# Sums' reciprocals and inverse norms of the attention layer: spread over channels by DMA from HBM instead of by matmuls

## The chip, the cores and the metric

The kernel runs on one core of one Trainium2 chip. A core has a tensor engine (PE in the profile, with its weight loads as PEld), a vector engine (DVE), a scalar engine (ACT), a general engine (POOL, GpSimd) and a queue processor that issues DMA transfers (SP). The metric is the device time of one execution in microseconds (us). All data is 32-bit floating point.

## The reference, cut to what matters

The network runs four layers over two images (batch 2) of 512 channels and 64 x 64 positions. Only the first layer is touched here. It is an attention with eight heads of 64 channels. Every position attends to its own 3 x 3 neighbourhood (nine "taps") and to 256 pooled tokens; queries and keys are scaled to unit length per head and position:

```python
q_norm = q / max(norm(q), 1e-12)                      # per head and position
q_scaled = (q_norm + query_embedding) * softplus(temperature)
k_l = k / max(norm(k), 1e-12)                         # per head and position
attn = softmax(concat([q_scaled . k_local (9 taps), q_scaled . k_pool (256 tokens)]))
a_local, a_pool = attn[..., :9], attn[..., 9:]
lt = q_norm @ learnable_tokens + learnable_bias + a_local
x_local = sum over taps of lt[tap] * v_local[tap]
x_pool = a_pool @ v_pool
out = (x_local + x_pool) @ W_proj + b_proj
```

Two kinds of numbers exist once per head and position and have to be multiplied onto all 64 channels of the head: the **inverse norms** of q and k, and the **reciprocal of the softmax's sum**, with which x_pool is scaled. Channels lie on the partitions (128 partitions are two heads), so each such number has to be brought from one row to 64 partitions. How that is done is what the change concerns.

## The kernel before

The first layer works on units: 128 channels (two heads) by 1024 positions, in two halves of 512 positions (TB). There are 4 x 4 = 16 units per image. A step `i` of the main loop works on several units in different stages at once. Each stage is a generator; `in_turn` runs every stage up to its next `yield`, in the order of the list, so a step is some ten "ticks" of interleaved work:

```python
for i in range(-4, units + 1):
    k, q, ahead, u, before = (unit(i + n) for n in (4, 3, 1, 0, -1))
    streams, ended = [], []
    stages = [self.norms(streams, ended)]
    if ahead is not None:
        stages.append(self.tap_products(ahead))     # DVE: q * shifted k, nine taps
    if u is not None:
        stages.append(self.attend(u))               # scores, exp, values, sums
    if before is not None:
        stages.append(self.weigh(before))           # nine taps of v, weighted
    if ahead is not None:
        stages.append(self.tap_sums(ahead))         # PE: sums over channels
    ...
    stages.append(self.projections(k, q, values, streams))   # ticks 6..9: k, k, q, q
    stages.append(self.normed(ended))               # inverse norms onto k and q
    ...
    in_turn(*stages)
```

`projections` writes the raw k or q (L2014) and its square (L2016) for four streams: k and q, two halves each. A step later `norms` sums the squares per head on PE, transposes them so that the positions lie on partitions, takes the inverse root on DVE in short instructions, and transposes back into `rows`, which holds the inverse norms of stream s in partitions 32 s and 32 s + 1:

```python
def norms(self, streams, ended):
    before, self.pending = self.pending, streams
    if not before:
        return
    yield
    ps = self.bank()
    for s in range(4):
        nc.tensor.matmul(ps[32 * s:32 * s + 32, :], self.cst[:, C_E32:C_E32 + 32],
                         before[s % len(before)][4], start=True, stop=True)       # L2048
    rows = wp.tile([P, TB], F32, name="n_rows")
    nc.scalar.copy(rows, ps)                                                      # L2051
    yield
    ...                            # L2055: transposes; L2062 to L2070: inverse root on DVE
    yield
    yield
    yield
    ps = self.bank()
    for t in range(NT):
        nc.tensor.transpose(ps[:, t * P:(t + 1) * P], self.wide[:, t, :], self.net.ident)  # L2076
    rows = wp.tile([P, TB], F32, name="n_rows")
    nc.scalar.copy(rows, ps)                                                      # L2078
    ended += [(s, rows[32 * s:32 * s + 2, :], *a) for s, a in enumerate(before)]
    yield
```

`normed` brings two rows onto 128 partitions with a matmul of contraction length 2 against a matrix of ones and zeros, and DVE multiplies k and q by the result in PSUM:

```python
def normed(self, ended):
    for _ in range(5):
        yield
    for which in "kq":
        mine = [(e, self.bank()) for e in ended if e[2] == which]
        for (s, rows, *_), ps in mine:
            nc.tensor.matmul(ps, self.cst[32 * s:32 * s + 2, C_ROW:C_ROW + P], rows,
                             start=True, stop=True)                               # L2090
        for (_, _, _, u, j, part, _), ps in mine:
            ...
            nc.vector.tensor_tensor(out, part, ps, ALU.mult)                      # L2098
        yield
    if mine:
        self.learned(mine[-1][0][3])     # L2111: PE on q, then ACT makes the scaled q
    yield
```

`attend` ends with the sums (L2205, L2209 on PE), their reciprocals (L2230), and the weights `el` of the taps, which go to HBM (`spread`, L2237) and come back one tap at a time, each row read onto 64 partitions (`fetch_tap`, L2247: two transfers of 256 KB per tap, into a ring of three `taps` buffers). `weigh` scales the pooled part by the reciprocals with the same kind of matmul, then works off nine taps:

```python
def weigh(self, u):
    out, R = self.out.pop(u), self.recip
    self.fetch_tap(2)
    yield
    banks = [self.bank() for _ in range(2)]
    for j, ps in enumerate(banks):
        q = slice(64 * j, 64 * j + 2)
        nc.tensor.matmul(ps, self.cst[q, C_ROW:C_ROW + P], R[q, :], start=True, stop=True)  # L2260
    for j, ps in enumerate(banks):
        o = out[:, j * TB:(j + 1) * TB]
        nc.vector.tensor_tensor(o, o, ps, ALU.mult)                               # L2263
    for k in range(9):
        ...
            nc.scalar.copy(ps, part)                                              # L2270
        ...
            nc.vector.tensor_tensor(part, vx (shifted), ps, ALU.mult)             # L2273
        nc.gpsimd.tensor_tensor(out, out, self.taps[k % 3], ALU.add)              # L2277
        if k + 3 < 9:
            self.fetch_tap(k + 3)
        if k < 8:
            yield
    nc.sync.dma_start(self.yd[:, cc, lo:lo + self.UT], out)                       # L2283
    yield
```

The PSUM tiles of all these parts come from one pool of five banks (`bank()`). All DMA of this layer is issued from one queue, in order, by SP.

Of the kernel before, what the change touches and what calls it, by code (L numbers as in the profile page):

```python
# [8 lines left out]
F32 = mybir.dt.float32  # L9
I32 = mybir.dt.int32  # L10
AF = mybir.ActivationFunctionType
ALU = mybir.AluOpType
# [3 lines left out]
P = 128  # L16
# [4 lines left out]
TB = 512  # L21
# [3 lines left out]
HD = 64  # L25
# [1674 lines left out]
class Local:  # L1700
# [9 lines left out]
    def __init__(self, net, X, Y, sp_scale, d, wp, yp, pp, ppt, pps):  # L1710
        self.net, self.nc, self.vec, self.cst = net, net.nc, net.vec, net.cst
        self.X, self.sp_scale, self.d = X, sp_scale, d
        self.wp, self.pp, self.ppt, self.pps = wp, pp, ppt, pps
        nc, new = self.nc, lambda shape, name: wp.tile(shape, F32, name=name)

        self.yd = yp.tile([P, KC, N], F32, name="yd")
        self.wd = yp.tile([3, P, KC, C], F32, name="wd")
        self.rows = cycle([yp.tile([P // 2, self.UT], F32, name=f"rows{i}") for i in range(2)]).__next__

        R = W + 2  # L1720
        self.kx_flat = flat = Y.rearrange("p k n -> p (k n)")
# [24 lines left out]
        self.w_sr = qs[:, :KC * C].rearrange("p (kc o) -> p kc o", kc=KC)  # L1746
        self.fold = flat[:, :6144].rearrange("p (i kc o) -> p i kc o", i=3, kc=KC)
        self.kp = new([P, KC, NK], "kp")
        self.vp = new([P, 2, C], "vp")
        self.qn = new([P, self.UT], "qn")  # L1750
        self.w3 = new([P, 3, KC, P], "w3")
        self.sq = [new([P, TB], f"sq{i}") for i in range(4)]
        self.half = new([P, 32], "mhalf32")
        self.wide = new([P, NT, P], "wide")
        self.qb = new([P, KC], "qe_scaled")
        self.bias = {i: new([P, KC], "b_" + i) for i in "qkv"}
        self.raw = {"k": self.kraw, "q": self.qn}
# [21 lines left out]
    def run(self):  # L1779
# [11 lines left out]
        for i in range(-4, units + 1):  # L1791
            k, q, ahead, u, before = (unit(i + n) for n in (4, 3, 1, 0, -1))
            streams, ended = [], []
            stages = [self.norms(streams, ended)]
            if ahead is not None:
                stages.append(self.tap_products(ahead))
            if u is not None:
                stages.append(self.attend(u))
            if before is not None:
                stages.append(self.weigh(before))  # L1800
            if ahead is not None:
                stages.append(self.tap_sums(ahead))

            values = ([ahead] if i >= self.UN - 1 and ahead is not None
                      else {-4: [0], -3: [1, 2], -2: [3]}.get(i, []))
            stages.append(self.projections(k, q, values, streams))
            stages.append(self.normed(ended))
            if i < -2:
                stages.append(islice(heads, 12 if i == -4 else None))
            if i == units - 3:  # L1810
                stages.append(self.fetch_output())
            if i > units - 3:
                stages.append(self.output(i - units + 2))
            in_turn(*stages)
# [223 lines left out]
    def norms(self, streams, ended):  # L2038


        nc, wp = self.nc, self.wp
        before, self.pending = self.pending, streams
        if not before:
            return
        yield
        ps = self.bank()
        for s in range(4):
            nc.tensor.matmul(ps[32 * s:32 * s + 32, :], self.cst[:, C_E32:C_E32 + 32],  # L2048
# [21 lines left out]
            nc.vector.scalar_tensor_tensor(dst, a, 1.5, y, ALU.add, ALU.mult)  # L2070
        yield
        yield
        yield
        ps = self.bank()
        for t in range(NT):
            nc.tensor.transpose(ps[:, t * P:(t + 1) * P], self.wide[:, t, :], self.net.ident)  # L2076
        rows = wp.tile([P, TB], F32, name="n_rows")
        nc.scalar.copy(rows, ps)  # L2078
        ended += [(s, rows[32 * s:32 * s + 2, :], *a) for s, a in enumerate(before)]
        yield  # L2080

    def normed(self, ended):

        nc = self.nc
        for _ in range(5):
            yield
        for which in "kq":
            mine = [(e, self.bank()) for e in ended if e[2] == which]
            for (s, rows, *_), ps in mine:
                nc.tensor.matmul(ps, self.cst[32 * s:32 * s + 2, C_ROW:C_ROW + P], rows, start=True,  # L2090
                                 stop=True)
            for (_, _, _, u, j, part, _), ps in mine:
# [5 lines left out]
                nc.vector.tensor_tensor(out, part, ps, ALU.mult)  # L2098
            yield
        if mine:  # L2100
            self.learned(mine[-1][0][3])
        yield

    def learned(self, u):
# [65 lines left out]
    def attend(self, u):  # L2170
# [64 lines left out]
        self.spread = self.rows()  # L2235
        for j in range(2):
            nc.sync.dma_start(self.spread[:, j * TB:(j + 1) * TB], el[j * HD:(j + 1) * HD, :])  # L2237
        self.fetch_tap(0)
        yield
        self.fetch_tap(1)  # L2240
        yield

    def fetch_tap(self, k):

        at = 32 * (k % 2) + 2 * k
        for h in range(2):
            self.nc.sync.dma_start(self.taps[k % 3][h * HD:(h + 1) * HD, :],  # L2247
                                   bcast(self.spread[at + h], 0, HD))

    def weigh(self, u):  # L2250

        nc = self.nc
        cc, y0 = u // self.UN, u % self.UN * self.UY
        out, R = self.out.pop(u), self.recip
        self.fetch_tap(2)
        yield
        banks = [self.bank() for _ in range(2)]
        for j, ps in enumerate(banks):
            q = slice(64 * j, 64 * j + 2)
            nc.tensor.matmul(ps, self.cst[q, C_ROW:C_ROW + P], R[q, :], start=True, stop=True)  # L2260
        for j, ps in enumerate(banks):
            o = out[:, j * TB:(j + 1) * TB]
            nc.vector.tensor_tensor(o, o, ps, ALU.mult)  # L2263
        for k in range(9):
            dy, dx = divmod(k, 3)
            parts = [self.taps[k % 3][:, j * TB:(j + 1) * TB] for j in range(2)]

            banks = [self.bank() for _ in range(2)]
            for ps, part in zip(banks, parts):
                nc.scalar.copy(ps, part)  # L2270
# [6 lines left out]
            nc.gpsimd.tensor_tensor(out, out, self.taps[k % 3], ALU.add)  # L2277
# [167 lines left out]
```

## Time and profile before

| | before |
|---|---|
| median of 3 runs | 5462.01 us (5449.31 to 5468.27) |
| span of the profiled execution | 5449.6 us |
| mean granted PE clock | 0.969 of full |
| one full step of the first layer (486.57 to 532.43, and the two after it) | 45.86 us each |
| first layer, first image | about 50 to 1100 us of the span |
| first layer, second image | about 2750 to 3800 us |

The page gives busy time per engine, the costliest groups of instructions by line, and the DMA queues. Below, the step of 45.86 us is read from the timeline: each row has its start, its length, the engine, the line of the kernel, the operation with output and input tiles, the count, and in brackets what the engine had been idle for. A 32-bit matmul of 512 columns leaves two matmul records, so a projection of four matmuls is a row of x8. Starts of successive rows on PE are the surer measure of what a row costs there, as the recorded ends are modelled.

### The profile page before, as it was taken

The page shows a single profiled execution, that of the slowest core. Times are in us where ns is not written, and L with a number is a line of the kernel's source. Part 1 is how long each engine was busy: PE and PEld are TensorE (multiplying, and loading weights), DVE is VectorE, ACT ScalarE, POOL GpSimd, SP SyncE. Part 2 cuts the span into 40 slices and gives each one's busy share as a digit, 9 for nine tenths or more (in the row PEclk, how much of TensorE's full clock was granted, in tenths as well). Part 3 has the DMA queues.
Part 4 walks back from the last instruction along what each step waited for, and adds up shares of the span by engine and source line. Part 5 has one row for each costly group of instructions (what it writes and reads, how often), then busy time and mean ns, then how long its engine had stood idle before and what let it go on. Part 6 is the DMA issues. An engine that isn't in the chain of part 4 may idle for free. (4 is left out here: it accounts for less than half of the span.)

```text
span 5449.6 us, 51666 instructions
## 1 busy us (share of the span) xinstructions
PE 5161.0 (95%) x18891; PEld 2254.2 (41%) x18891; DVE 3144.7 (58%) x3918; ACT 1793.0 (33%) x3409; POOL 1803.2 (33%) x1198
## 2 busy tenths in 40 slices
PE   7999999999988899999999999998999889999998
PEld 4423332554333344544444333335543334445443
DVE  3256667745679633565532566676456895334565
ACT  1245555233212233212212455542432131332221
POOL 0025556401310045444400355554012101554443
PEclk9999999999989999999989999999999899999999
DMA  3024445500000000211110344455000000000111
GB/s 141 2 62 122 128 126 154 153 18 24 1 1 0 1 1 1 82 35 57 51 55 2 81 126 125 124 154 154 1 24 0 1 0 1 1 8 20 38 36 42
DMA packets 113563, 293.27 MB, mean 54 GB/s; under 512 B 17234, under 2 KB 30034, under 8 KB 111252
## 3 DMA queue, kind: packets, MB, share of 16 engines
q1 hardware_dynamic: 113300, 289.88, 18.1%
q8 instruction: 151, 2.47, 0.2%
q14 instruction: 112, 0.92, 0.1%
HBM read 241.32 MB, written 48.50 MB: 53 GB/s over the span
## 5 line engine op out<-in xcount | busy, mean ns | idle before, releaser
L133 PE MATMUL mm<-big,w 128*128 128x512 f32 x2560 | 1188.4, 609 | 5.2 <-DVE late L2230 5.1
L133 PEld LDWEIGHTS mm<-big,w 128*128 128x128 f32 x2560 | 467.8, 191 | 687.4 <-issue 590.3
L2277 POOL TENSOR_TENSOR late<-late,big 128x1024 f32<-128x1024 f32 x192 | 454.7, 2368 | 298.6 <-DVE big L2273 285.3
L1265 POOL TENSOR_TENSOR total<-prob 128x512 f32<-128x512 f32 x128 | 159.6, 1269 | 759.3 <-ACT prob L1262 759.3
L1182 PE MATMUL acc<-big,dg 128*128 128x512 f32 x704 | 320.0, 613 | 59.0 <-DVE big L697 25.9
L1624 POOL TENSOR_SCALAR qf_sum<-qf,ksum_ratio 128x512 f32<-128x512 f32 x128 | 198.8, 1562 | 511.1 <-ACT qf L1674 353.8
L1437 POOL TENSOR_TENSOR big<-big 128x512 f32<-128x512 f32 x224 | 277.8, 1271 | 235.0 <-ACT big L1428 235.0
L2198 POOL TENSOR_TENSOR late<-late 128x512 f32<-128x512 f32 x128 | 160.6, 1276 | 487.1 <-ACT late L2187 448.2
L697 DVE TENSOR_TENSOR big<-big 128x3968 f32<-128x3968 f32 x72 | 308.8, 4289 | 6.9 <-ACT big L698 0.9
L2273 DVE TENSOR_TENSOR big<-big,mm 128x512 f32<-128x512 f32 x384 | 254.7, 679 | 85.1 <-ACT mm L2270 84.3
L1428 ACT ACTIVATE big<-mm,ed 128x256 f32<-128x256 f32 x512 | 193.7, 488 | 276.5 <-DVE top L1424 248.8
L2270 ACT COPY mm<-big 128x512 f32<-128x512 f32 x384 | 220.6, 594 | 161.4 <-DMA big<-rows 123.7
L1362 PE MATMUL mm<-proj,k 64*128 64x256 f32 x2048 | 268.9, 393 | 0.9 <-ACT k L1329 0.9
L1282 DVE RECIPROCAL recip<-psD 128x512 f32<-128x512 f32 x64 | 214.9, 3357 | 87.2 <-PE psD L1279 87.2
L1655 PE MATMUL mm<-k,w 128*128 128x512 f32 x512 | 242.0, 612 | 14.1 <-DVE k L1648 14.1
L1583 DVE TENSOR_REDUCE tops<-mm 128x2 f32<-128x512 f32 x256 | 161.5, 684 | 160.2 <-PE mm L1362 159.9
L1262 ACT ACTIVATE prob<-mm 128x512 f32<-128x512 f32 x256 | 132.0, 605 | 364.4 <-PE mm L1259 359.2
L1362 PEld LDWEIGHTS mm<-proj,k 64*128 64x128 f32 x2048 | 206.5, 188 | 105.7 <-issue 90.1
L2138 DVE TENSOR_TENSOR prod<-qs,big 128x1024 f32<-128x1024 f32 x192 | 230.5, 1215 | 30.7 <-PE tap L2151 29.1
L2277 POOL TENSOR_TENSOR late<-late,tap 128x1024 f32<-128x1024 f32 x96 | 226.5, 2360 | 64.4 <-DVE tap L2273 45.7
L133 PE MATMUL mm<-big,big 128*128 128x512 f32 x512 | 238.9, 629 | 0.0
L2151 PE MATMUL tap<-prod,cst 128*32 128x512 f32 x768 | 226.7, 612 | 9.9 <-DVE prod L2138 9.8
(364 smaller groups left out, 8300.2 us busy)
## 6 DMA issues: line engine op xcount, KB each, us to landing
big<-rows SPq DMA_DIRECT2D x384, 256.0 KB
tap<-rows SPq DMA_DIRECT2D x192, 256.0 KB
yd<-late SPq DMA_DIRECT2D x32, 512.0 KB
lost_all<-lost SPq DMA_DIRECT2D x128, 128.0 KB
out<-big SPq DMA_DIRECT2D x64, 256.0 KB
big<-in_W_kv SPq DMA_DIRECT2D x8, 1024.0 KB
rows<-late SPq DMA_DIRECT2D x64, 128.0 KB
big<-yd SPq DMA_DIRECT2D x16, 512.0 KB
```

Of the source, the lines that this page charges most:

```text
L133: self.nc.tensor.matmul(ps, w[:, kc, :], X[:, kc, blk * TB:(blk + 1) * TB], start=(kc == 0), stop=(kc == KC - 1))
L697: nc.vector.tensor_tensor(o, a, b, ALU.max)
L1182: nc.tensor.matmul(accs[b], dg, src[:, b * TB:(b + 1) * TB], start=(j == 0), stop=(j == 6))
L1282: nc.vector.reciprocal(r, psD)
L1362: nc.tensor.matmul(pS[h][i][:, t, :], k[lo:lo + HD, tok:tok + P], proj[lo:lo + HD, :], start=True, stop=True)
L1437: nc.gpsimd.tensor_tensor(a, a, part, ALU.add)
L1655: nc.tensor.matmul(ps, self.wo[:, kc, oc * P:(oc + 1) * P], qs[:, kc, :], start=(kc == 0), stop=(kc == KC - 1))
L2138: self.nc.vector.tensor_tensor(self.prods[k % 3].rearrange("p (y x) -> p y x", x=W), qs, self.kx[:, y + dy:y + dy + self.UY, dx:dx + W], A ...
L2151: nc.tensor.matmul(ps[32 * q:32 * q + 32, :], self.cst[:, C_TAPW + 16 - 2 * k:C_TAPW + 48 - 2 * k], self.prods[k % 3][:, j * TB:(j + 1) * ...
L2270: nc.scalar.copy(ps, part)
L2273: nc.vector.tensor_tensor(part.rearrange("p (y x) -> p y x", x=W), self.vx[:, y:y + self.UY // 2, dx:dx + W], ps.rearrange("p (y x) -> p y ...
L2277: nc.gpsimd.tensor_tensor(out, out, self.taps[k % 3], ALU.add)
```

## The change

The row-to-64-partitions matmuls are replaced by the way that the tap weights already take: out to HBM, and back with each row read onto 64 partitions, then an ACT copy into the same PSUM bank from which DVE multiplies.

For the reciprocals no write is added. Row 20 + h of what is already written to `spread` holds exp(0) times the reciprocal plus zero, which is the reciprocal of head h. So the reciprocals become a tenth "tap", numbered 0, and the nine taps become 1 to 9. For the norms there is a new HBM buffer `roots` of 2 x 4 x 512 numbers (two of them in turn); the read-back lands in the `sq` buffers, whose squares have been used by then. The norms' stage starts without its first `yield` and has one `yield` less before the second transposes, and it now stands after the projections in a tick instead of at the front. The load of the last weights into `sq` is moved to a later tick, as `sq` is in use for longer. It is meant to take work off PE.

```diff
+        self.roots = cycle([yp.tile([2, 4, TB], F32, name=f"roots{i}") for i in range(2)]).__next__
-        self.sq = [new([P, TB], f"sq{i}") for i in range(4)]
+        self.squares = new([P, 4, TB], "sq")
+        self.sq = [self.squares[:, i, :] for i in range(4)]
 ... run
-            stages = [self.norms(streams, ended)]
+            stages = []
 ...
-            stages.append(self.normed(ended))
+            stages += [self.norms(streams, ended), self.normed(ended)]
 ... fetch_output
-        for _ in range(3):
+        for _ in range(7):
             yield
 ... norms
-        yield
         ps = self.bank()
         for s in range(4):
 ...
         yield
         yield
-        yield
         ps = self.bank()
         for t in range(NT):
 ...
-        ended += [(s, rows[32 * s:32 * s + 2, :], *a) for s, a in enumerate(before)]
+        roots = self.roots()
+        for h in range(2):
+            nc.sync.dma_start(roots[h], rows[h:P:32, :])
+        for s in range(0, len(before), 2):
+            for h in range(2):
+                nc.sync.dma_start(self.squares[h * HD:(h + 1) * HD, s:s + 2, :],
+                                  bcast(roots[h, s:s + 2], 0, HD))
+        ended += [(self.sq[s], *a) for s, a in enumerate(before)]
 ... normed
-            for (s, rows, *_), ps in mine:
-                nc.tensor.matmul(ps, self.cst[32 * s:32 * s + 2, C_ROW:C_ROW + P], rows, start=True,
-                                 stop=True)
+            for (root, *_), ps in mine:
+                nc.scalar.copy(ps, root)
 ... fetch_tap
-        at = 32 * (k % 2) + 2 * k
+        at = 32 * ((i - 1) % 2) + 2 * (i - 1) if i else 20
+        t = self.taps[(10 * u + i) % 3]
 ... weigh
-        out, R = self.out.pop(u), self.recip
-        self.fetch_tap(2)
-        yield
-        banks = [self.bank() for _ in range(2)]
-        for j, ps in enumerate(banks):
-            q = slice(64 * j, 64 * j + 2)
-            nc.tensor.matmul(ps, self.cst[q, C_ROW:C_ROW + P], R[q, :], start=True, stop=True)
-        for j, ps in enumerate(banks):
-            o = out[:, j * TB:(j + 1) * TB]
-            nc.vector.tensor_tensor(o, o, ps, ALU.mult)
-        for k in range(9):
+        out = self.out.pop(u)
+        self.fetch_tap(u, 2)
+        for i in range(10):
 ...
             for ps, part in zip(banks, parts):
                 nc.scalar.copy(ps, part)
+            dy, dx = divmod(i - 1, 3)
             for j, (ps, part) in enumerate(zip(banks, parts)):
+                if i == 0:
+                    o = out[:, j * TB:(j + 1) * TB]
+                    nc.vector.tensor_tensor(o, o, ps, ALU.mult)
+                    continue
 ...
-            nc.gpsimd.tensor_tensor(out, out, self.taps[k % 3], ALU.add)
-            if k + 3 < 9:
-                self.fetch_tap(k + 3)
-            if k < 8:
+            if i:
+                nc.gpsimd.tensor_tensor(out, out, t, ALU.add)
+            if i + 3 < 10:
+                self.fetch_tap(u, i + 3)
+            if i < 9:
                 yield
```

More of the change, by code (lines that the diff above doesn't have):

```diff
@@ L2087, in normed @@
         for which in "kq":
-            mine = [(e, self.bank()) for e in ended if e[2] == which]
-            for (s, rows, *_), ps in mine:
-                nc.tensor.matmul(ps, self.cst[32 * s:32 * s + 2, C_ROW:C_ROW + P], rows, start=True,
-                                 stop=True)
-            for (_, _, _, u, j, part, _), ps in mine:
+            mine = [(e, self.bank()) for e in ended if e[1] == which]
+            for (root, *_), ps in mine:
+                nc.scalar.copy(ps, root)
+            for (_, _, u, j, part, _), ps in mine:
                 out = part
@@ L2100, in normed @@
         if mine:
-            self.learned(mine[-1][0][3])
+            self.learned(mine[-1][0][2])
         yield
@@ L2237, in attend, with fetch_tap @@
             nc.sync.dma_start(self.spread[:, j * TB:(j + 1) * TB], el[j * HD:(j + 1) * HD, :])
-        self.fetch_tap(0)
+        self.fetch_tap(u, 0)
         yield
-        self.fetch_tap(1)
+        self.fetch_tap(u, 1)
         yield
-    def fetch_tap(self, k):
-        at = 32 * (k % 2) + 2 * k
+    def fetch_tap(self, u, i):
+        at = 32 * ((i - 1) % 2) + 2 * (i - 1) if i else 20
+        t = self.taps[(10 * u + i) % 3]
         for h in range(2):
-            self.nc.sync.dma_start(self.taps[k % 3][h * HD:(h + 1) * HD, :],
-                                   bcast(self.spread[at + h], 0, HD))
+            self.nc.sync.dma_start(t[h * HD:(h + 1) * HD, :], bcast(self.spread[at + h], 0, HD))
     def weigh(self, u):
@@ L2253, in weigh @@
         cc, y0 = u // self.UN, u % self.UN * self.UY
-        out, R = self.out.pop(u), self.recip
-        self.fetch_tap(2)
-        yield
-        banks = [self.bank() for _ in range(2)]
-        for j, ps in enumerate(banks):
-            q = slice(64 * j, 64 * j + 2)
-            nc.tensor.matmul(ps, self.cst[q, C_ROW:C_ROW + P], R[q, :], start=True, stop=True)
-        for j, ps in enumerate(banks):
-            o = out[:, j * TB:(j + 1) * TB]
-            nc.vector.tensor_tensor(o, o, ps, ALU.mult)
-        for k in range(9):
-            dy, dx = divmod(k, 3)
-            parts = [self.taps[k % 3][:, j * TB:(j + 1) * TB] for j in range(2)]
+        out = self.out.pop(u)
+        self.fetch_tap(u, 2)
+        for i in range(10):
+            t = self.taps[(10 * u + i) % 3]
+            parts = [t[:, j * TB:(j + 1) * TB] for j in range(2)]
             banks = [self.bank() for _ in range(2)]
```

## The prediction

> **What bounds the kernel now.** I read the engines' busy times first, then found one full step of the first layer in PE's timeline (the same row, L2183, recurs after 45.86 us), then laid a table of three such steps.
>
> ```profile
> PE 5161.0 (95%) x18891; PEld 2254.2 (41%) x18891; DVE 3144.7 (58%) x3918; ACT 1793.0 (33%) x3409; POOL 1803.2 (33%) x1198
> ```
>
> ```profile
> core 0: us, PE busy (x) PEld busy (x) DVE busy (x) ACT busy (x) POOL busy (x), PEclk, DMA share, GB/s
> 486.57:532.43 45.86, 45.74 (x166) 14.78 (x165) 31.60 (x50) 25.88 (x45) 26.22 (x13) 1.00 0.46 119
> 532.43:578.29 45.86, 45.74 (x166) 14.76 (x165) 31.61 (x50) 25.81 (x45) 26.21 (x13) 1.00 0.45 125
> ```
>
> The step repeats to 0.01 us, PE has no hole in it, and every other engine has 14 us or more to spare; DMA is at 0.46. So a step is as long as PE's queue. The rows of PE around the norms and sums show it row by row (two stretches of one step):
>
> ```profile
> 505.80 0.65 PE L2076 MATMUL mm<-cst,wide 128*128 128x128 f32 x4
> 506.39 1.94 PE L2193 MATMUL mm<-late,vp 128*64 128x512 f32 x8
> 508.25 1.13 PE L2090 MATMUL mm<-n_rows,cst 2*128 2x512 f32 x4
> 509.31 1.06 PE L2151 MATMUL tap<-prod,cst 128*32 128x512 f32 x6
> 510.30 3.70 PE L133 MATMUL mm<-big,w 128*128 128x512 f32 x8
> 513.93 1.13 PE L2090 MATMUL mm<-n_rows,cst 2*128 2x512 f32 x4
> 514.99 1.94 PE L2205 MATMUL mm<-late,cst 128*64 128x512 f32 x8
> 516.86 1.08 PE L2209 MATMUL mm<-late,cst 64*64 64x512 f32 x4
> ...
> 539.17 1.13 PE L2260 MATMUL mm<-late,cst 2*128 2x512 f32 x4
> 540.41 0.66 PE L2055 MATMUL mm<-cst,n_rows 128*128 128x128 f32 x4
> ```
>
> The reader takes the distance of starts: the pair L2090 costs 1.06 us (508.25 to 509.31, and 513.93 to 514.99), the pair L2260 1.24 us (539.17 to 540.41). A projection L133 costs 3.63 us.
>
> For the waits that could replace this, I read SP's and ACT's timelines and waits (the stretch 400 to 850 us, about ten steps):
>
> ```profile
> 523.30 1.10 SPq L2237 DMA_DIRECT2D rows<-late  x2
> 526.31 1.10 SPq L2247 DMA_DIRECT2D big<-rows  x2
> ...
> 515.02 0.45 SPq L2247 DMA_DIRECT2D big<-rows  x1
> 515.52 0.59 SPq L2247 DMA_DIRECT2D big<-rows  x1
> ...
> 519.61 0.59 ACT L2270 COPY mm<-big 128x512 f32<-128x512 f32 x1 [0.71 <-DMA big<-rows]
> ```
>
> ```profile
> SPq L2247 <- POOL late L2277: 242.0, 68, 13.4
> ACT mm L2270 <- DMA big<-rows: 13.6, 16, 1.8
> ```
>
> A write to HBM holds the read behind it for 3.0 us (523.30 to 526.31). A tap of 512 KB (two transfers) is usable 4.6 us after its first issue (515.02 to 519.61). SP mostly waits for POOL to free a tap buffer, and ACT hardly waits for taps: 13.6 us in ten steps.
>
> **What the Trainium skill says.** "TensorE: Matmul & The Clock Gate", Part 3, says that matmuls with few rows run at the same time when they sit in different row groups. The trace agrees: two matmuls of L2090 take 1.06 us together, while one full matmul of a projection takes about 0.86 (a row of x16, two projections, spans 7.06 us for eight). So I count pairs, not instructions. "TensorEngine Tiling (Array Packing)", Key Properties, says that changing the tiling mode drains the engine. The trace fits: that double projection (7.06) is 0.20 us shorter than twice 3.63. So each pair taken out also takes out a switch, which the distances of starts hold already; the move of L2076 from between two other shapes to just behind a projection of the same shape saves one more. "DMA: Bandwidth & Descriptors", Two DMAs through the same engine are not ordered, says that the read of something just written must wait for the write's completion; the 3.0 us above are that wait. "ScalarE: Activation LUTs", What ACT_TABLE_LOAD costs, gives 186 ns + 0.833 ns per element for an activation without pointers, 613 ns for 512; the trace has 591 ns for the copy L2270, and two in a row in 1.11 us.
>
> **The change, part by part, for a full step.**
> - Removed from PE: two pairs L2090 (2 x 1.06 = 2.12 us), one pair L2260 (1.24), and one switch by the move of L2076 (0.2). Sum 3.56 us of 45.86, all of it on the path.
> - Added on ACT: six copies of 128 x 512, in pairs of 1.11 us, so 3.3 us. ACT goes from 25.9 to about 29.2 us of a step, and has gaps of 3 us in front of most projections' results. Beside other work.
> - DVE: as many multiplications as before. Those with the reciprocals move one tick forward, into a hole: L2263 used to wait 10.2 us for PE.
> - DMA: one more tap (512 KB) and the norms' read-back of four transfers (4 streams x 128 partitions x 2 KB = 1 MB), beside nine taps (4.7 MB). The share rises to about 0.46 x 6.2/4.7 x 45.9/43 = 0.65. Beside other work, but everything lands later.
> - Queue of SP: two writes and four reads of 0.55 us each, and the wait of 3 us between, in which no tap can be issued. Taps are fetched three ticks ahead, so this should be covered.
>
> So much if no new wait comes. The **new chain** of the norms is what I doubt. From the start of L2076: transposes 0.65, ACT copy to 1.6 (0.6 and some queue), write and wait 3.0, then k's half landed 4.6 later, so at 9.2 us; two copies and two multiplications of k, then q's half, landed some 2 us after k's: copied at 12.5, multiplied at 14. `learned` (L2111) needs that q. On PE, from the start of L2076 to L2111 the new order has L2076 0.6, scores L2183 1.06, taps 1.0, values 1.86, taps 1.0, projection 3.63, sums 1.87 and 1.0, projection 3.63: 15.6 us. That is 1.6 us more than the chain needs, so `learned` itself just passes. But the k copies wait in ACT's queue until 9.2, and PE reaches L2205 at 9.2 too (0.6 + 1.06 + 1.0 + 1.86 + 1.0 + 3.63). L2205 needs one of five banks, and those are then held by two k copies, two tap copies and a projection, all behind the same ACT queue. If the tap copies stand behind k's, the first bank comes free at about 10.8 us (1.1 for k, 0.6 for the tap, then DVE). I put the stall at 0 to 2 us, 1.3 in the mean, and choose to lose that.
>
> Sum over the span: steps 3 to 12 of each image are full (20 steps): 20 x (3.56 - 1.3) = 45 us. Steps 0 to 2 (6 steps) carry no projection of v, and PE waits for DVE there (prod by L2138), so I count 1.2 us each: 7 us. In the three start-up steps the ticks are short, and the chain of 12 to 14 us has little to hide behind; against 2 to 3 us removed I count a loss of 1 us each: -6 us. In the last four steps L2260 goes (1.2 us each), but ACT already waits for tap transfers there (48.8 us between 880 and 1120), and the tenth tap lengthens that: no gain counted. Together about -46 us, so 5462 - 46 = 5416 us.
>
> **Rivals.**
> 1. *PE stays the only bound.* Then nothing stalls: 26 steps x 3.56 = 93 us, and some from the start-up and the end: about 5365. For it: no engine is near full, and taps are hardly waited for. Against it: the norms' round trip has slack near zero.
> 2. *The round trip through HBM becomes the bound of the step.* SP works in order; if the writes stand behind a tap waiting for POOL, or the read-back meets two taps in flight, k lands 3 to 6 us later, ACT stands still, banks run out, and PE waits longer than it saves. For it: SP waits for POOL 24 us in a step, and taps come 2.4 us apart from POOL. Against it: L2076 comes before the fourth tick, and one tap buffer is usually fetched before. It would make 5480 to 5540.
> 3. *DMA bandwidth.* Share 0.65 in the steps, 0.7 already at the end (1000 to 1050 us: 0.71). If taps come late throughout, the end and start-up lose 10 us per image: 5420 to 5440 instead of 5416. It can go along with either.
> 4. *The inverse root on DVE is late.* Before, it ended at 503.68, and PE would now want it at about 502.5. DVE is 1.2 us lighter ahead of it, so I expect under 1 us of wait; it is inside the 1.3.
>
> **Range and chances.** Rival 1 sets the low end, somewhat softened (5365); a moderate rival 2 the high one (5480). Over 2% faster is under 5353 us: this needs all 3.56 us in every one of 32 steps (114 us) and no loss, nearly excluded, 0.03. Over 2% slower is above 5571: a stall of about 7 us in every step, 0.04. Between, faster is likelier than slower, as the removed work is certain and on the path.
>
> **What would show it.** In the changed profile the step between recurring L2183 rows should be 43 to 44.5 us; the rows of PE with 2 x 512 inputs gone but for those of the pooled tokens; ACT with six copies more in a step; DMA share about 0.65. A hole in PE ahead of L2205 or L2111, with ACT waiting for the read-back, shows the chain. Nothing lost there: rival 1. Holes over 4 us a step: rival 2. Wrong would be most of all my choice of 1.3 us, and the order in which the copies stand in ACT's queue, which the source does not fix: the trace of before has a tap copy of the next tick ahead of the scores' exponentials.

## The result, and the profile after

| | before | after |
|---|---|---|
| median, same session, 4 runs each | 5459.13 us (5449.31 to 5468.27) | 5662.70 us (5655.80 to 5664.63) |
| ratio, 95% interval | 1 | **1.0371** [1.035, 1.0392] |
| span of the profiled execution | 5449.6 us | 5660.7 us |
| one full step, mean of 480 to 880 us | 45.46 us | 53.64 us |
| PE idle in such a step | 0.1 us | 8.5 us |

The change makes the kernel slower by 3.7%; the prediction was a little faster, and its range ends at 5480. The matmuls did go, and PE has less to do. First the engines' line of the page of the changed kernel, then its table for one full step, from one row L2213 (the sums, L2205 before) to the next:

```profile
PE 5124.6 (91%) x18507; PEld 2253.0 (40%) x18507; DVE 3187.2 (56%) x3918; ACT 1887.4 (33%) x3601; POOL 1808.0 (32%) x1198
```

```profile
core 0: us, PE busy (x) PEld busy (x) DVE busy (x) ACT busy (x) POOL busy (x), PEclk, DMA share, GB/s
601.87:654.45 52.58, 44.80 (x153) 14.82 (x153) 33.44 (x51) 28.57 (x52) 26.45 (x13) 0.95 0.58 141
```

384 matmul records fewer on PE, 192 copies more on ACT, and still 211 us more span. In the step, PE is busy for 44.80 of 52.58 us where it had been for 45.74 of 45.86, and no other engine is near full either. So nothing is full: something waits. PE's timeline (idle before a row and its releaser in brackets) says where:

```profile
627.58 1.12 PE L2191 MATMUL mm<-big,kp 64*128 64x512 f32 x2
629.07 1.09 PE L2191 MATMUL mm<-big,kp 64*128 64x512 f32 x2 [0.37 <-DVE late L2276]
...
639.35 0.60 PE L2077 MATMUL mm<-cst,wide 128*128 128x128 f32 x4
...
645.80 3.70 PE L133 MATMUL mm<-big,w 128*128 128x512 f32 x8 [1.95 <-DVE big L2279]
654.45 3.48 PE L2213 MATMUL mm<-late,cst 128*64 128x512 f32 x8 [4.94 <-DVE tap L2279]
657.86 1.07 PE L2217 MATMUL mm<-late,cst 64*64 64x512 f32 x4
```

The large hole lies ahead of L2213, where the prediction said that it would lie if the chain of the norms was late. The releaser is DVE's work on a tap (L2279), that is, the freeing of a PSUM bank; L2213 reads nothing of it. Of the 8.5 us of idle in the mean step, 5.8 stand here; of the rest 2.0 stand ahead of projections and 0.6 ahead of the scores. Two smaller things are to be seen. L2213 itself lasts 3.4 us from start to start (654.45 to 657.86) where it cost 1.87 before. And the scores L2191, a pair of heads side by side before, come in two halves of 1.1 us when the second half has to wait for a bank that tap 0 (L2276, the reciprocals) holds.

DVE waits for ACT, and ACT's copies wait for SP's transfers. ACT's timeline, then DVE's, SP's and one row of POOL's (start, length, line, tiles, count):

```profile
640.13 0.58 ACT L2079 COPY n_rows<-mm 128x512 f32<-128x512 f32 x1
...
651.89 1.11 ACT L2099 COPY mm<-sq 128x512 f32<-128x512 f32 x2 [6.00 <-DMA sq<-roots]
652.93 1.10 ACT L2271 COPY mm<-tap 128x512 f32<-128x512 f32 x2
654.31 1.11 ACT L2099 COPY mm<-sq 128x512 f32<-128x512 f32 x2 [0.27 <-DMA sq<-roots]
```

```profile
652.51 1.29 DVE L2106 TENSOR_TENSOR big<-big,mm 128x512 f32<-128x512 f32 x2 [6.76 <-ACT mm L2099]
653.71 1.28 DVE L2279 TENSOR_TENSOR tap<-big,mm 128x512 f32<-128x512 f32 x2
```

```profile
640.83 1.09 SPq L2257 DMA_DIRECT2D tap<-rows  x2
641.98 0.59 SPq L1996 DMA_DIRECT2D w<-wd  x1
642.61 1.09 SPq L2083 DMA_DIRECT2D roots<-n_rows  x2
645.93 0.48 SPq L2257 DMA_DIRECT2D big<-rows  x1
646.51 2.45 SPq L2086 DMA_DIRECT2D sq<-roots  x4
```

```profile
643.55 2.35 POOL L2284 TENSOR_TENSOR late<-late,big 128x1024 f32<-128x1024 f32 x1 [2.75 <-DVE big L2279]
```

Read together, this is the large hole. The rows are ready at 640.71 (ACT). SP first issues a tap and a weight load, and the write at 642.61. The read-back is issued at 646.51, behind half a tap, and that half tap (645.93) went out when POOL's sum ended (645.90) and freed its buffer. Such a half tap stands between write and read-back in all eight steps from 477 to 868 us. ACT stands still for 6.00 us at the copy of k's norms. The copies of the next tap stand behind it in ACT's queue (issued at 640.83, copied at 652.93), so DVE gets that tap only then, and the banks that PE needs for L2213 come free after DVE's first half of it.

What a step of PE costs, by starts of rows without idle, before and after:

| | before | after | difference |
|---|---|---|---|
| spreading matmuls L2090, L2260 | 3.30 | 0 | -3.30 |
| tap sums | 6.75 | 5.98 | -0.77 |
| scores (L2183, now L2191) | 4.23 | 5.82 | +1.59 |
| sums (L2205, now L2213) | 1.87 | 3.56 | +1.69 |
| second sums (L2209, now L2217) | 1.01 | 1.31 | +0.30 |
| projections L133 | 21.33 | 21.57 | +0.24 |
| other rows | 6.86 | 6.91 | +0.05 |
| idle | 0.12 | 8.49 | +8.37 |
| step | 45.46 | 53.64 | +8.18 |

Over the span, I take the starts of a unit's last transfer (L2283, now L2290) as marks. From the first to the twelfth such mark an image takes 585 and 586 us instead of 501 and 502: +84 each, 168 together. The way to the first mark (in the first image from the start of the span, in the second from the last mark of the first) takes 11 and 10 us more, the last four steps 7 and 10 us more. That is 206 of the 211 us between the two spans.

### The profile page after: what moved, and what is told of

It reads as the page before. It is cut to its first block, busy times and chain, and to the rows that moved or that the text cites. A ratio compares the mean times of both kernels' runs of the same rounds, so it can differ in the third digit from the quotient of the medians.

```text
span 5660.7 us, 51585 instructions
## 1 busy us (share of the span) xinstructions
PE 5124.6 (91%) x18507; PEld 2253.0 (40%) x18507; DVE 3187.2 (56%) x3918; ACT 1887.4 (33%) x3601; POOL 1808.0 (32%) x1198
## 5 line engine op out<-in xcount | busy, mean ns | idle before, releaser
L133 PE MATMUL mm<-big,w 128*128 128x512 f32 x2560 | 1189.9, 611 | 75.1 <-DVE big L2279 25.9
L133 PEld LDWEIGHTS mm<-big,w 128*128 128x128 f32 x2560 | 473.5, 193 | 759.3 <-issue 590.8
L2279 DVE TENSOR_TENSOR big<-big,mm 128x512 f32<-128x512 f32 x384 | 253.2, 679 | 136.4 <-ACT mm L2271 128.2
L2271 ACT COPY mm<-big 128x512 f32<-128x512 f32 x428 | 243.3, 591 | 215.3 <-DMA big<-rows 166.3
L1655 PE MATMUL mm<-k,w 128*128 128x512 f32 x512 | 242.3, 613 | 15.3 <-DVE k L1648 15.3
L133 PE MATMUL mm<-big,big 128*128 128x512 f32 x512 | 239.5, 631 | 0.0
L2213 PE MATMUL mm<-late,cst 128*64 128x512 f32 x256 | 102.6, 947 | 146.3 <-DVE big L2279 89.4
```

The source lines that it names most:

```text
L133: self.nc.tensor.matmul(ps, w[:, kc, :], X[:, kc, blk * TB:(blk + 1) * TB], start=(kc == 0), stop=(kc == KC - 1))
L1655: nc.tensor.matmul(ps, self.wo[:, kc, oc * P:(oc + 1) * P], qs[:, kc, :], start=(kc == 0), stop=(kc == KC - 1))
L2279: nc.vector.tensor_tensor(part.rearrange("p (y x) -> p y x", x=W), self.vx[:, y:y + self.UY // 2, dx:dx + W], ps.rearrange("p (y x) -> p y ...
```

## The experiments

Each kernel is one edit of the kernel before or of the changed one; ratios are to the kernel before in the same session. "Step" and "idle" are PE's, as in the table above. One caution holds for all: the compiler orders each engine's instructions anew for every kernel, so an edit can change more than it says.

**The two halves.** e1_recip_only takes the tenth tap alone, e2_norms_only the norms by HBM alone.

```diff
 e1: before, with this part of the change only
-            nc.tensor.matmul(ps, self.cst[q, C_ROW:C_ROW + P], R[q, :], start=True, stop=True)
+        for i in range(10):          # tap 0: the reciprocals, by spread and fetch_tap
 e2: the change, with the weigh and fetch_tap of before
```

> Only the reciprocals go by HBM (the tenth tap); norms as before, with their matmuls and in their old place. Theory 'round trip': the loss of the whole change comes from the norms' read-back, so this part alone saves the pair L2260 (1.24 us in each of 32 units, at most 40 us): 5415 to 5440 us, full step near 44.7 us. Rival 'tenth tap': the longer row of taps starves ACT and the tap ring, so most of the loss of 204 us is here: above 5600 us.

> Only the norms go by HBM; the reciprocals keep their matmul. Theory 'round trip': all of the loss, and the 1.24 us of L2260 back in each step: 5670 to 5710 us, full step near 53.5 us. Rival 'tenth tap': 5380 to 5440 us.

e1: 5429.0 us, **0.9965** [0.9954, 0.9976], step 43.81, idle 0.4. e2: 5595.52 us, 1.0262 [1.0245, 1.0279], step 51.95, idle 5.4. The half with the reciprocals does what the prediction said of it and is faster than both kernels. The other half loses, by less than expected: -21 and +146 make +125, the whole change +204. The halves are not additive; together they cost some 79 us more.

**Is it the wait of the copies?** Three kernels with the whole change. e3_ready keeps all transfers, but the four norm copies of a unit read a constant tile (k and q are then scaled by constants, not by their norms); the other two of the six copies that the change adds are tap 0's, and stay. e4_direct has no norm copies: DVE multiplies straight from the fetched rows. e10_still keeps the copies and their wait for the transfers, but the transfers read an HBM buffer written once at the start (again constants in place of the norms), so that they need not wait for the write.

```diff
 e3
-                nc.scalar.copy(ps, root)
+                nc.scalar.copy(ps, self.cst[:, :TB])
 e4
-            mine = [(e, self.bank()) for e in ended if e[1] == which]
-            for (root, *_), ps in mine:
-                nc.scalar.copy(ps, root)
+            mine = [(e, e[0]) for e in ended if e[1] == which]
 e10
-                                  bcast(roots[h, s:s + 2], 0, HD))
+                                  bcast(self.still[h, s:s + 2], 0, HD))
```

> The whole change, but the four norm copies of a unit read a constant tile that is always there, instead of the read-back; all transfers are still made. (k and q are scaled by constants: this part of the computation is left out.) Theory 'round trip': it is the wait of ACT for the read-back that costs, so without it PE's saving shows: step 42.5 to 44 us, 5360 to 5420 us. Rival 'bandwidth': the added 1.5 MB per step slow the taps, wait or no wait: above 5550 us.

> The whole change, but DVE multiplies k and q straight from the read-back in SBUF: no ACT copies of the norms and no PSUM banks for them. Theory 'round trip by way of ACT's queue and the banks': ACT no longer stands still, so tap copies and projections get past; DVE stands in its place, which has more idle time, so most of the loss goes: 5420 to 5560 us. Rival 'plain latency': if the chain up to the scaled q alone sets the step, it stays within 20 us of 5663.

> The whole change with copies that do wait for their read-back, but the reads come from a buffer written once at the start, so they can be issued long before they are needed. (k and q are scaled by constants.) Theory 'lateness': six ACT copies, their banks and the 1.5 MB more per step cost nothing when the data is there in time: step 44 to 45 us, 5420 to 5460 us. Rival 'banks and ACT': the copies themselves starve PE: 5520 us or more.

e10: 5466.69 us, 1.0023 [1.0014, 1.0032], step 45.3, idle 2.2, just above the range of its theory. All copies, banks and bytes are still there; what is gone is that the read must follow this step's write, and with it the whole chain from the norms to the read. Some 190 of the 204 us go with that. The waits of ACT between 500 and 900 us (total, times, longest), first of the changed kernel, then of e10:

```profile
ACT mm L2099 <- DMA sq<-roots: 49.3, 11, 7.4
```

```profile
ACT mm L2102 <- DMA sq<-still: 3.0, 3, 1.2
```

And SP's queue in e10, the write and two of the four reads:

```profile
628.40 1.07 SPq L2086 DMA_DIRECT2D roots<-n_rows  x2
629.57 1.13 SPq L2089 DMA_DIRECT2D sq<-still  x2
```

These two reads follow 1.2 us behind the write, where it was 3.9 (642.61 to 646.51); the other two go out 14 us before the write (614.11), so the data is early and not only 2.7 us sooner. The six copies themselves cost little.

e3: 5522.9 us, 1.0133 [1.0116, 1.015], step 49.5, idle 4.2. Between the two expectations: two thirds of the loss go with the wait, 73 us stay. e4: 5645.02 us, 1.035 [1.0333, 1.0368], step 54.0, idle 8.0: far from the theory, and within the 20 us of the changed kernel that the rival 'plain latency' had named. The wait changes the engine. One wait of DVE and one of ACT in e4 between 500 and 900 us, then a row of PE:

```profile
DVE big L2104 <- DMA sq<-roots: 20.2, 5, 5.4
...
ACT big L2017 <- DVE big L2104: 50.7, 7, 7.6
```

```profile
650.05 1.92 PE L2157 MATMUL tap<-big,cst 128*32 128x512 f32 x4 [4.63 <-DVE big L2144]
```

DVE now meets the late read-back at the multiplication L2104, and ACT stands behind DVE. PE no longer waits ahead of the sums (L2211 here). Of its idle, 4.3 us a step stand ahead of tap sums, whose products need the scaled q, and 3.0 us ahead of `learned`, which needs q. So the copies and their banks are not needed for the loss: without them the longer way up to the scaled q costs as much. How much of that is bare latency and how much DVE's other work in between is not shown. In the changed kernel it is the bank that holds PE, as L2213 reads neither k nor q.

**What of the round trip is left in e3?** All five kernels here scale k and q by constants. e5_small reads back 16 columns instead of 512, still behind the fresh write. e6_no_hold reads at full size, from the buffer written once. e9_reads_later issues the reads a tick after the writes, behind the next tap. e14_no_trip issues neither writes nor reads. e15_pinned_ready fixes SP's order: writes, reads, taps as in the source.

```diff
 e5 (on e3)
-                nc.sync.dma_start(self.squares[h * HD:(h + 1) * HD, s:s + 2, :],
-                                  bcast(roots[h, s:s + 2], 0, HD))
+                nc.sync.dma_start(self.squares[h * HD:(h + 1) * HD, s:s + 2, :16],
+                                  bcast(roots[h, s:s + 2, :16], 0, HD))
 e6 (on e3): roots -> self.still in the reads, as in e10
 e9 (on e3)
+        yield                         # between the writes and the reads
 e14 (on e3)
-        for h in range(2):
-            nc.sync.dma_start(roots[h], rows[h:P:32, :])
-        ...                           # and the reads
 e15 (on e3): keep_in_program_order around the transfers of norms and fetch_tap
```

> As the run before with ready copies, and the four reads of a unit bring 16 columns instead of 512 (1/32 of 1 MB); the write and the wait of the queue for it stay. (k and q scaled by constants.) Theory 'data': the 1 MB delays the taps, so most of the 7 us per step between this step of 49.4 us and PE's own 42.3 goes: 43 to 45.5 us, 5370 to 5440 us. Rival 'held queue': taps are late because SP stands at the reads until the write has landed: stays at 5500 to 5530 us.

> As the run before with ready copies, but the four reads of a unit, of full size, come from a buffer written once at the start, so SP never waits for a write at them; the write of the norms is still made. (k and q scaled by constants.) Theory 'data': stays at 5490 to 5530 us. Rival 'held queue': 5380 to 5440 us.

> Ready copies as before (k and q scaled by constants), all transfers of full size, but the four reads are placed a tick after the writes, behind the next tap's fetch, so SP finds the write landed. Theory 'held queue': the step goes from 49.5 us to about 44.3 and the time to 5400 to 5450 us. Rival 'the two together are only an accident of order' or 'data': 5490 us or more.

> The whole change with its six norm copies, but these read a constant tile, and neither the write of the inverse norms nor their read-back is issued (k and q get a constant factor in place of the norms). e3_ready, which kept the transfers, still stood 73 us above the kernel before. Theory A (those 73 us are the queue of SP held for the write, and the full-size reads on the DMA engines): 5380 to 5430 us, step 43 to 44.5 us. Rival (they come from the other order in which the instructions stand after the move, as in e7_move_only): 5490 to 5540 us, tap sums on PE near 8 to 10 us a step.

> e12_pinned (on SP the writes, the reads and the taps stand in the order of the source) with norm copies that read a constant tile, so nothing on ACT waits for the read-back. Theory A (the held queue costs e3 its 73 us by itself): 5500 to 5540 us as e3_ready, since the queue is held as long. Rival (in e3 it was the accidental order of transfers and of the tap sums): under 5460 us, with tap sums at 6 to 7 us a step.

| | us | ratio, 95% interval | step | idle | tap sums |
|---|---|---|---|---|---|
| e14: no write, no read | 5426.35 | 0.9954 [0.9938, 0.997] | 44.6 | 1.7 | 5.9 |
| e5: waits for the write, small reads | 5424.1 | 0.9952 [0.9939, 0.9965] | 44.3 | 1.6 | 5.8 |
| e6: full reads, not behind the write | 5443.44 | 0.9988 [0.9977, 0.9999] | 44.2 | 1.5 | 6.4 |
| e9: full reads, a tick later | 5481.12 | 1.0039 [1.0025, 1.0053] | 46.7 | 3.3 | 7.9 |
| e3: full reads behind the write | 5522.9 | 1.0133 [1.0116, 1.015] | 49.5 | 4.2 | 8.4 |
| e15: as e3, order on SP fixed | 5574.78 | 1.0227 [1.0197, 1.0258] | 51.3 | 5.9 | 8.4 |

e14 settles one question: with the stage moved, the copies and the tenth tap in place, but no round trip, the kernel is faster than before. The whole loss hangs on the round trip. e5 and e6 settle another: neither the hold of SP's queue alone nor the full-size reads alone cost much. So e5 came out as the theory 'data' had it and e6 3 us above the range of the rival 'held queue', and neither of the two explains e3 by itself; e9 lies between its two. And the way by which e3 pays is not that of the changed kernel. Waits of DVE for the tap sums and of ACT for a tap between 500 and 900 us, of e3, then of e14:

```profile
DVE prod L2146 <- PE tap L2159: 40.3, 7, 8.5
...
ACT mm L2271 <- DMA big<-rows: 19.8, 13, 2.9
```

```profile
DVE big L2139 <- PE tap L2152: 8.0, 10, 1.4
...
ACT mm L2264 <- DMA big<-rows: 44.8, 18, 6.1
```

In e3, ACT waits less for taps than in the faster e14. What has grown is that DVE's products wait for PE's tap sums, and these cost 8.4 us a step, against 5.9. PE's rows right behind the second sums, of e3, then of e14:

```profile
601.56 1.07 PE L2217 MATMUL mm<-late,cst 64*64 64x512 f32 x4
605.37 1.92 PE L2159 MATMUL tap<-big,cst 128*32 128x512 f32 x4 [2.73 <-DVE big L2146]
```

```profile
593.42 1.07 PE L2210 MATMUL mm<-late,cst 64*64 64x512 f32 x4
594.43 3.70 PE L133 MATMUL mm<-big,w 128*128 128x512 f32 x8
```

In three of the seven steps of e3 from 498 to 845 us tap sums stand there and wait for DVE's product; in e14 a projection follows in every step from 501 to 816. The source order of this work is the same in both kernels, so the compiler's order differs. That all of the 73 us come from it is not shown. e15 was to fix this by fixing the order on SP; it came out slower than e3, beyond both expectations, with the products waiting even more. How e3's 73 us divide stays open. In the changed kernel itself the tap sums are at 5.98, so that this loss is not part of its 204 us.

**Can the chain be started sooner, ended later, or put in order?** e7_move_only is the kernel before with only the move of the norms' stage, no transfer. e8_later is the change with `normed` a tick later, ahead of the projections. e12_pinned is the change with SP's order fixed (no half tap between write and read). e13_sooner has the second transposes a tick sooner. All four compute everything.

```diff
 e7 (on before): norms behind projections, its first yield and one later yield out
 e8 (on the change)
-        for _ in range(5):
+        for _ in range(6):            # and normed listed ahead of projections
 e12 (on the change): keep_in_program_order around the transfers of norms and fetch_tap
 e13 (on the change)
-        yield
         yield
         ps = self.bank()              # second transposes
```

> The kernel before with only the order changed: the norms' stage last in a tick and one yield less, all matmuls kept, no new transfer. Theory 'round trip': the order alone is worth nothing or a switch of 0.2 us in 32 steps: 5435 to 5460 us. Rival 'order': if the new order puts the inverse root or the transposes in PE's way, above 5480 us.

> The whole change, with the multiplication of k and q by the norms one tick later (before the projections of that tick, which overwrite them), so the read-back has some 5 us more. Theory 'round trip': ACT's wait of 6 to 7 us per step falls to 1 to 2 us, and the step from 53.5 to 48 to 50 us, the level of the run with ready copies: 5490 to 5550 us. Rival 'plain latency' up to the scaled q: the wait only moves along, above 5630 us.

> The whole change with SP's order pinned: the two writes, the four reads, then the next tap, so no read stands behind a tap that waits for POOL. Theory 'length of the round trip': the read-back lands 1 us sooner, the step loses 1 us, the next tap comes later: 5600 to 5650 us. Rival 'it is the half tap in front of the reads': below 5520 us.

> The whole change with the second transposes, and so the round trip, one tick (2 to 4 us) sooner. Theory 'length of the round trip': the step falls by 2 to 3 us, 5560 to 5610 us. Rival: PE then waits for the inverse root of DVE at these transposes and nothing is won: within 20 us of 5653.

e8: 5616.91 us, 1.0303 [1.0278, 1.0327]; e12: 5624.54 us, 1.0307 [1.0282, 1.0332]; e13: 5699.53 us, 1.0436 [1.0419, 1.0454]. PE's idle per step is 6.3, 6.9 and 8.4 us: less in e8 and e12, but most of the wait moves along. In e8 most of it (5.1) stands ahead of a projection that waits for ACT. In e12 the half tap is gone from between, and SP's waits between 500 and 900 us now list the write:

```profile
SPq L2086 <- DMA roots<-n_rows: 19.1, 8, 3.2
```

The changed kernel has no such row, as SP stood at the half tap meanwhile. In the mean of eight steps the read-back of e12 goes out 3.6 us behind the write instead of 4.9, k's copy comes 10.9 us after the transposes instead of 12.7, and the hole ahead of the sums is 3.9 us instead of 5.9. So the half tap makes about a third of the hole, and the rest stays with no half tap between; the kernel gains 38 of the 204 us. e13's rows of PE and SP:

```profile
645.43 0.63 PE L2076 MATMUL mm<-cst,wide 128*128 128x128 f32 x4 [1.01 <-DVE wide L2072]
...
648.30 1.08 SPq L2082 DMA_DIRECT2D roots<-n_rows  x2
652.02 0.48 SPq L2256 DMA_DIRECT2D tap<-rows  x1
652.61 3.26 SPq L2085 DMA_DIRECT2D sq<-roots  x4
```

From the transposes to the reads it is 7.2 us, as in the changed kernel (639.35 to 646.51), with half a tap between here too. The sooner start does shrink the hole ahead of the sums, to 4.1 us a step. But the transposes now wait 1.0 us for DVE's inverse root in every step, as the rival had it, and the tap sums cost 7.9 us instead of 6.0, with 2.0 us of waiting ahead of them. e8 and e13 missed what I expected of them; e12 met it.

e7: 5526.05 us, 1.0138 [1.0116, 1.0159], step 50.0 with only 1.1 us idle, though it does the same work as before. Rows of its PE timeline:

```profile
655.11 1.05 PE L2149 MATMUL tap<-big,cst 128*32 128x512 f32 x4 [0.17 <-DVE big L2136]
656.34 1.05 PE L2149 MATMUL tap<-prod,cst 128*32 128x512 f32 x4 [0.18 <-DVE prod L2136]
```

Each tap's sums stand alone, 1.23 us apart, paced by DVE's product; before, the sums of two taps often ran together (in 1.00 us from 497.08 to 498.08). The tap sums cost 10.0 us a step instead of 6.75. I had expected the move to cost nothing. It costs 78 us here, and e14, with the same move and another order, is faster than before. So I take it for a cost of the order, not of the move.

**The better version taken further.** e11_direct_recip is e1 with tap 0 multiplied by DVE straight from SBUF.

```diff
-            banks = [self.bank() for _ in range(2)]
+            banks = [self.bank() for _ in range(2)] if i else parts
```

> e1_recip_only (reciprocals by HBM, norms as before), but DVE multiplies the pooled part straight with the fetched reciprocals in SBUF, without the two ACT copies and the two banks per unit. If banks and ACT matter little once nothing waits: as e1, 5420 to 5440 us. If two fewer banks in use per unit let taps run further ahead: 5400 to 5420 us.

5473.23 us, 1.0039 [1.0025, 1.0052]: less work, and slower than e1. A wait of DVE between 500 and 900 us goes with it:

```profile
DVE late L2269 <- DMA big<-rows: 36.3, 5, 7.3
```

DVE now stands for the transfer up to 7.3 us at a time, with everything behind it; in e1 no wait of ACT for a tap was over 2.9 us. As in e4, the direct path puts the wait on the busier queue. The step is 46.1 us instead of 43.8; 1.0 us of this is tap sums, 0.6 idle, 0.5 scores. Whether a changed order has a part in it is not shown. **e1_recip_only is the best version run that computes everything**: 0.9965 [0.9954, 0.9976], a small gain but clear of noise.

## Why the prediction was wrong

**The step that failed is the size of the stall**: "I put the stall at 0 to 2 us, 1.3 in the mean". The hole ahead of the sums measured 5.8 us in the mean step, with 2.0 us of slower sums behind it (L2213 and L2217). Of the other 2.7 us of idle, e14, which has no round trip, shows 1.7 as well. The mechanism is the prediction's own second rival, "The round trip through HBM becomes the bound of the step", down to the place of the hole, and its bound for that ("Holes over 4 us a step") was passed. Its 5480 to 5540 was too low as well. Term by term, counted from the start of the second transposes, in the step shown (639.35) and in the mean of the eight steps from 477 to 868 us:

| term | predicted | step shown | mean of eight |
|---|---|---|---|
| rows copied at | 1.6 | 1.4 | 1.4 |
| write issued at | 1.6 | 3.3: a tap and a weight load first | 2.3 |
| write to read | 3.0 | 3.9: half a tap between | 4.9 |
| read to k usable | 4.6 | 5.4 | 5.5 |
| sum to k | 9.2 | 12.5 | 12.7 |
| k to a free bank | 1.6 | 2.6 | 2.6 |
| L2213 starts at | 10.8 | 15.1 | 15.3 |
| PE ready for L2213 at | 9.2 | 10.1, of it 1.95 idle | 9.4 |

PE was ready when the prediction said; the trip came 4.5 us too late. The term that was mis-sized most is **write to read, 3.0 us, measured 4.9**: half a tap stands between, and it waits for POOL to free its buffer, in seven of the eight steps. The prediction had this case in its second rival and set against it that one tap buffer is usually fetched before. The other three errors are of about one us, in a chain that the prediction itself gave "slack near zero", and all have the same sign. That a read must wait until the write before it is complete is what "DMA: Bandwidth & Descriptors" of the Trainium skill asks for (Two DMAs through the same engine are not ordered); e12, with no half tap between, has 3.6 us from write to read. The estimate took both transfers from quiet places of the old trace and the queue of SP as empty. With that, "Taps are fetched three ticks ahead, so this should be covered" was the wrong question: what was not covered was ACT, with tap copies behind the norm copies. And the reading "ACT hardly waits for taps: 13.6 us" counted one name of the tap buffers; the other (`tap`) adds 3.5 us, which changes nothing.

**What the stall drags along** was not in the sum at all. Behind the hole PE ran at about half its clock, as this row of the window table of the changed kernel says, with its columns as above:

```profile
654.45:657.90 3.45, 3.45 (x10) 0.81 (x10) 1.76 (x3) 2.58 (x4) 2.36 (x1) 0.54 0.56 124
```

PE is busy throughout, with a granted clock of 0.54. "TensorE: Matmul & The Clock Gate" (Part 1, What's actually happening) of the Trainium skill says that the clock falls to half after an idle window of about 3.4 us; the holes of 4.9 and 6.2 us with L2213 at 3.4 and 3.6 us behind them agree. So does e2, where the holes ahead of the sums are 3.0 us at most and the sums cost 1.87 us. The prediction had no term for this.

The other points:

- **Removed from PE, 3.56 us**: right; the rows are gone, 3.30 us of the mean step. But e14 says what it was worth: with no round trip at all its step is 44.55, only 0.9 us shorter, as the scores come apart (5.74 instead of 4.23) and 1.7 us of idle appear. So the changed kernel's slower scores (+1.59) come without the round trip too, and the first rival's 5365 was out of reach even without one (e14: 5426.35).
- **ACT 29.2 us a step**: 28.7 in the mean of seven steps. Right.
- **DMA share 0.65**: 0.56 in those steps, as they are longer. The bytes were right: 138 GB/s over 53.6 us against 126 over 45.5 is 1.29 times as much, predicted 6.2/4.7 = 1.32. Bandwidth (third rival) bounds nothing here.
- **Inverse root late (fourth rival)**: no wait for it in the step shown; L2077 follows the projection at once.
- **Order in ACT's queue**: the guess "If the tap copies stand behind k's" came true.
- **Start-up -6 us, end 0**: measured a loss of about 10 us an image at the start and 7 to 10 at the end, against 3 us an image predicted at the start and nothing at the end. Right in sign, wrong in size; in part it is the longer trip again, in part the tenth tap, as e1's last four steps of the first image take 183 us instead of 177.
- **Reciprocals**: 1.24 us a step from L2260; e1's step is 1.65 shorter. Right, and the only part of the change that gained with the norms still computed.

## What to carry to other kernels

Before a matmul of 1 us is replaced by a trip through HBM, lay the whole trip, with all that stands ahead of it in the issuing queue and with the write's completion, beside the time in which the result is wanted; if the slack is near zero, count on losing. Data that lies in HBM already (the reciprocals, written for the taps anyway) can take that way, data made in the same step lost here. And ask what else stands behind the waiting instruction in its engine's queue: the late data cost nearly the same on ACT (1.0371) and on DVE (1.0350).

## What the runs showed that I had not expected

- After holes of 4.9 to 6.3 us PE's next rows cost nearly double (L2213: 3.4 to 3.6 us instead of 1.87), so that a hole costs about a third more than its length.
- Against the kernel with no round trip (0.9954), the wait for the write with small reads adds nothing (0.9952), full-size reads without that wait add 0.3% (0.9988), and both together 1.8% (1.0133), although no copy waits for the data. I had expected two costs that add. PE's order differs too, so this is not shown to be the transfers' doing alone.
- The same instructions in another order cost 1.4% (e7), by tap sums of one tap instead of two at a time.
